# An early expert's result behind the last routing, and expert weights asked for first

## The chip, the cores and the metric

The kernel runs on one core of a Trainium2 chip. A core has a matrix engine (TensorE, PE in the profile; its weight loads are listed as PEld), a vector engine (DVE), a scalar engine (ACT) that evaluates exponents, Gelu and tanh and also copies, a general engine (POOL) that here does small arithmetic and issues the indirect DMAs, and a queue engine (SP) that issues the plain DMAs one after another. Each engine works through its own queue in order, and waits on semaphores for the others. The metric is the device time of one execution in microseconds; lower is better.

## What is computed

Sixteen elements of 112 tokens with 256 features pass through two layers, each an attention and a mixture of eight experts:

```python
x = x + _L0_xattn_ref(_layernorm(x), ctx_1024, ctx_1024, mask, wq, wk, wv, wo)   # 16 heads
x = x + _L0_ffn_ref(_layernorm(x), wr, w1, b1, w2, b2)      # top 2 of 8, capacity 560 an expert
x = x + _L1_xattn_ref(_layernorm(x), ctx_1024, ctx_1024, mask)                 # one head
x = x + _L1_ffn_ref(_layernorm(x), gate_w, w1, w2, w3)      # top 2 of 8, no capacity
```

The change concerns the end of the first attention and the first expert stage. There each token's logits pick two experts; a token's place in an expert's list is the count of earlier tokens that chose it; an expert computes `gelu(x @ w1 + b1) @ w2 + b2` on its rows, and each row's result is weighted by its gate and added to its token.

## The kernel before, in words

All matrix products are in float32. A matmul call of the source shows as two matmuls in the profile.

**First attention with routing beside it.** The work is cut into 64 steps, four for each of the 16 elements; a step does four heads: scores (L712), row minimum (`least`, L720), exponent (`exps`, L727), transposes of the exponents (`turn`, L733 to L739), product with the values (`weigh`, L749). A step's scores, its transposes and its values are done in successive steps, so the pipeline drains in steps 64 and 65. Everything else is hung into the steps by `put(step, place, function, arguments)` (L779): `place` 0, 1 or 2 is one of three points within a step, and functions at the same point run in the order in which they were put. For PE, ACT and DVE this order is fixed by hand (`tc.manual_schedule`, L823). POOL and SP are ordered by the framework's planner, which weighs program order against its own estimate of when operands are there.

After the heads of element b, in steps counted from 4b: `queries_first` (6), `heads_first` (7), `output` (8: output product, residual sum into `x`, statistics and reciprocal standard deviation), `normed2` (9), `routing_T` (10), `logits` and `first_two` (11). Then, for groups of elements (`GROUPS0`; the last two groups are element 14 and element 15 alone), `route_a` (12: one-hot choices and running counts `macc`, tanh of the gate on ACT), `gates` and `route_b` (13: positions by two matmuls, L244 and L245), `to_slots` (13: `dest`, then two indirect scatters of the normalised rows, with gate and token number behind each row, into the experts' slots `xg`). The reciprocal standard deviation is found by three Newton steps (`rstd_of`, L165), on POOL for elements 0 to 14 and on DVE for element 15.

**The early expert.** When ten elements are routed, the least chosen expert is fixed as the first one (`early_choice`). Its first 256 slots are filled by then; step 57 loads them with that expert's bias and weights (`early_loads`), step 64 transposes them (`early_T`), step 65 works out gates (`early_gates`). `early_hidden(f)` computes one of eight chunks of the hidden layer, two of them in each of the steps 66 to 69, and `early_result(j, f0, n)` half of one of two 128-row result tiles, in steps 70 to 73. A finished tile gets its bias and gate on DVE and is added to the tokens by an indirect DMA on POOL.

**The end of the stage.** After the steps, `macc` is summed (`ps_n`, L872), and `in_order` (L301) sorts the remaining experts by their counts: `ids0`, `idn0` (their numbers, read by SP into registers at L299) and the capacities. `terms` (L876) gathers the biases in that order.

**Expert stage.** Pools of this stage (`fp`, `fw`, L884) take the room of those of the attention; `wpool` spans both. The loop at L979 runs over eight experts. For expert `at` it asks SP for the next one's rows and bias (`slots0`, L891), then `w1` and `w2`; it turns its own rows (L913, L914), computes hidden products (`hidden0`, L942) for one or two parts of the rows, and after each part the result of the part before (`result0`, L959 to L964, then an indirect add on POOL). Weights have two buffers for each of `w1` and `w2`: experts with an even number in `wpool`, with an odd one in `fw`. The bias `b2` has two buffers as well. In this stage the planner orders all engines. A load of rows waits until all scatters have landed.

The second layer follows, with an attention and eight experts of its own; the change does not touch its code.

Of the kernel before, what the change touches and what calls it, by code (L numbers as in the profile page):

```python
# [8 lines left out]
F32 = mybir.dt.float32  # L9
# [9 lines left out]
B, S, S2, D = 16, 112, 375, 256  # L19
# [3 lines left out]
FC = F // 128  # L23
# [10 lines left out]
ST = 128  # L34
# [22 lines left out]
def xattn_ffn_kernel(ctx: ExitStack, tc: tile.TileContext, a: dict, out: bass.AP):  # L57
# [107 lines left out]
    def rstd_of(mv, n, pool=False):  # L165

        v = small.tile([S, n], F32, tag=f"var{n}", name="var")
        nc.vector.tensor_scalar(v, mv[:, :, 1], EPS, None, ALU.add)
        r = small.tile([S, n], F32, tag=f"rstd{n}", name="rstd", bufs=4)
        nc.vector.tensor_scalar(r.bitcast(I32), v.bitcast(I32), 1, None, ALU.arith_shift_right)  # L170
        nc.vector.tensor_scalar(r.bitcast(I32), r.bitcast(I32), -1.0, float(0x5F3759DF), ALU.mult, ALU.add)  # L171
        t = small.tile([S, n], F32, tag=f"newton{n}", name="newton")
        if pool:
            for _ in range(3):
                nc.gpsimd.tensor_tensor(t, r, r, ALU.mult)  # L175
                nc.gpsimd.tensor_tensor(t, t, v, ALU.mult)
                nc.gpsimd.tensor_scalar(t, t, -0.5, 1.5, ALU.mult, ALU.add)
                nc.gpsimd.tensor_tensor(r, r, t, ALU.mult)
            return r
        nc.vector.tensor_scalar(v, v, -0.5, None, ALU.mult)  # L180
        for _ in range(3):
            if n == 1:
                nc.vector.scalar_tensor_tensor(t, r, r, v, ALU.mult, ALU.mult)
            else:
                nc.vector.tensor_tensor(t, r, r, ALU.mult)
                nc.vector.tensor_tensor(t, t, v, ALU.mult)
            nc.vector.scalar_tensor_tensor(r, t, 1.5, r, ALU.add, ALU.mult)
        return r
# [154 lines left out]
    with tc.tile_pool(name="aw", bufs=1) as aw, tc.tile_pool(name="ea", bufs=1) as ea, tc.tile_pool(name="ap", bufs=2) as ap, tc.tile_pool(  # L343
# [200 lines left out]
        def output(b):  # L544
            oT = oTs.pop(b)
            ps = bank("ps_o")
            for k in range(KC):
                nc.tensor.matmul(ps[:S, :D], oT[:, k, :], wo[:, k, :], start=(k == 0), stop=(k == KC - 1))
            nc.vector.tensor_tensor(x[:, b, :], ps[:S, :D], x[:, b, :], ALU.add)
            based.append(nc.sync.dma_start(out=xd[b * S : (b + 1) * S, :], in_=x[:, b, :]).ins)  # L550
            mv = small.tile([S, 1, 2], F32, tag="mv2", name="mv2")
            stats(mv, 0, x[:, b, :])
            xn2[b] = mv, rstd_of(mv, 1, b + 1 < B)

        def normed2(b):
            mv, rstd = xn2[b]
# [222 lines left out]
        def put(step, place, f, *args):  # L779
            beside.setdefault((step, place), []).append((f, args))  # L780

        for b in range(B):
            if b:
                at = NG * (b - 1)
                put(at, 0, context_T, b)
                put(at + 1, 0, key_T, b, 0)
                put(at + 1, 2, value, b, 2, 1)
                put(at + 2, 0, key_T, b, 1)
                if b % QB == 0:
                    put(at - 2, 0, layer_norm1, b // QB)  # L790
                    put(at - 1, 0, normed1, b // QB)
                    put(at, 2, query_n, b // QB)
                    put(at + 3, 0, query_T, b // QB)
                put(at + 3, 1, value, b, 0, 2)
            at = NG * b
            put(at + 6, 1, queries_first, b)
            put(at + 7, 2, heads_first, b)
            put(at + 8, 1, output, b)
            put(at + 9, 1, normed2, b)
            put(at + 10, 0, routing_T, b)  # L800
            put(at + 11, 0, logits, b)
            put(at + 11, 1, first_two, b)
        for g, (t0, n) in enumerate(GROUPS0):
            at = NG * (t0 + n - 1) + 12
            put(at, 1, route_a, g)
            put(at + 1, 0, gates, g)
            put(at + 1, 2, route_b, g)
            for j in range(n):
                put(at + 1 + (j if n > 2 else 0), 2, to_slots, t0 + j)
# [3 lines left out]
        put(STEPS - 7, 2, early_loads)  # L813
        put(STEPS, 2, early_T)
        put(STEPS + 1, 2, early_gates)
        for f in range(FC):
            put(STEPS + 2 + f // 2, 2, early_hidden, f)
        for j in range(CAPA // ST):
            for i in range(2):
                put(STEPS + 6 + 2 * j + i, 2, early_result, j, i * FC // 2, FC // 2)  # L820

        engines = {mybir.EngineType.PE, mybir.EngineType.Activation, mybir.EngineType.DVE}
        with tc.manual_schedule(engines=engines):  # L823
            nc.vector.tensor_scalar(nmask, nmask, -1.0, None, ALU.mult)
            layer_norm1(0)
            normed1(0)
            context_T(0)
            key_T(0, 0)
            key_T(0, 1)
            query_n(0)  # L830
            query_T(0)
            value(0, 0, 2)
            value(0, 2, 1)
            got, was = None, None
            for step in range(max(at for at, _ in beside) + 1):

                def place(i):
                    for f, args in beside.get((step, i), ()):
                        f(*args)

                now, was, got = step < STEPS, got, None
                if now:
                    got = scores(step)
                    least(got, 0)
                    least(got, 1)
                if was:
                    turn(step - 1, was, 0)
                if now:
                    exps(got, 0)
                place(0)  # L850
                if now:
                    exps(got, 1)
                    least(got, 2)
                    least(got, 3)
                back = 2 <= step < STEPS + 2
                if back:
                    weigh(step - 2, 0)
                    weigh(step - 2, 1)
                if was:
                    turn(step - 1, was, 1)  # L860
                if now:
                    exps(got, 2)
                place(1)
                if now:
                    exps(got, 3)
                if back:
                    weigh(step - 2, 2)
                if was:
                    turn(step - 1, was, 2)
                place(2)  # L870
            ps = bank("ps_n")
            nc.tensor.matmul(ps[:, :E], ones_, macc[:, B, :], start=True, stop=True)  # L872
            at = in_order(small, ps[:, :E], CAP, caps8[:, 0, :], ids0, idn0, over0, capof0, pick0)
            full = [128, E // 2, FC, E]
            for r in (slice(0, E // 2), slice(E // 2, E)):
                terms = ap.tile(full, F32, tag="s", name="terms", bufs=8)  # L876
                nc.vector.tensor_tensor(
                    terms, at[:, r].unsqueeze(2).to_broadcast(full),
                    b1T.rearrange("p e k -> p k e").unsqueeze(1).to_broadcast(full), ALU.mult,
                )  # L880
                nc.vector.tensor_reduce(b1s[:, r], terms, AX.X, ALU.add)


    with tc.tile_pool(name="fp", bufs=2) as fp, tc.tile_pool(name="fw", bufs=2) as fw, tc.tile_pool(  # L884
# [6 lines left out]
        def slots0(e, r0, rows, own=""):  # L891

            xs = fp.tile([ST, -(-rows // ST) if own else NT, W], F32, tag="xs" + own, name="xs", bufs=1 if own else 2)
            src = of_expert(xg[0:ROWS, :].rearrange("(e r) d -> e r d", e=E), e)
            full = rows // ST
            load = nc.sync.dma_start(
                out=xs[:, :full, :], in_=src[r0 : r0 + full * ST, :].rearrange("(j p) d -> p j d", p=ST)
            )
            after_scatters("xg", load)
            if rows > full * ST:  # L900
                load = nc.sync.dma_start(out=xs[: rows - full * ST, full, :], in_=src[r0 + full * ST : r0 + rows, :])
                after_scatters("xg", load)
            b2 = fp.tile([ST, D], F32, tag="b2" + own, name="b2", bufs=1 if own else 2)
            of = slice(e, e + 1) if isinstance(e, int) else bass.ds(e, 1)
            nc.sync.dma_start(out=b2, in_=a["L0_ffn_b2"][of, :].to_broadcast([ST, D]))
            return xs, b2
# [72 lines left out]
        for at in range(E):  # L979
# [1 line left out]
            todo = CAPS0[at] if at else (CAPB,)  # L981
            rows = sum(todo)
            if at + 1 < E:
                nxt = slots0(who[at + 1], 0, sum(CAPS0[at + 1]))
                pool = wpool if at % 2 else fw
                w1_next = w_in(a["L0_ffn_w1"], who[at + 1], "w1", pool, at + 1)
                w2_next = w_out(a["L0_ffn_w2"], who[at + 1], "w2", pool, at + 1)
            gate, token = weights_of(xs, rows, lambda m: ids0[:m, at : at + 1] if at else idf0[:m])
            xsT = turned0(xs, rows)
# [464 lines left out]
```

## Time and profile before

| what | us |
|---|---|
| median of 3 runs (1166.43 to 1173.64) | 1169.13 |
| profiled execution, its own time | 1165.95 |
| its span, first to last instruction | 1164.2 |
| PE busy, of the span | 1059.8 (91%) |
| DVE, ACT, POOL busy | 476.4, 385.7, 274.6 |
| mean granted PE clock, of full speed | 0.961 |

In the timeline rows of the profile, the first two numbers are the start and the length of a stretch in microseconds from the span's start. Then come the engine, the line of the kernel, the operation, what it writes and reads, the sizes, and how many instructions were merged. Brackets give the engine's idle time before them and what ended it. SPq marks the queue of SP. In rows of the form start:end, the engines' busy times (PE, PEld, DVE, ACT, POOL, with instruction counts) are followed by the granted PE clock, the share of time that the DMA engines were busy, and GB/s. Matmuls are pipelined, so that a busy PE isn't PE at its peak.

### The profile page before, as it was taken

The page shows a single profiled execution, that of the slowest core. Times are in us where ns is not written, and L with a number is a line of the kernel's source. Part 1 is how long each engine was busy: PE and PEld are TensorE (multiplying, and loading weights), DVE is VectorE, ACT ScalarE, POOL GpSimd, SP SyncE. Part 2 cuts the span into 40 slices and gives each one's busy share as a digit, 9 for nine tenths or more (in the row PEclk, how much of TensorE's full clock was granted, in tenths as well). Part 3 has the DMA queues.
Part 4 walks back from the last instruction along what each step waited for, and adds up shares of the span by engine and source line. Part 5 has one row for each costly group of instructions (what it writes and reads, how often), then busy time and mean ns, then how long its engine had stood idle before and what let it go on. Part 6 is the DMA issues. An engine that isn't in the chain of part 4 may idle for free. (4 is left out here: it accounts for less than half of the span.)

```text
span 1164.2 us, 17046 instructions
## 1 busy us (share of the span) xinstructions
PE 1059.8 (91%) x6262; PEld 734.0 (63%) x6262; DVE 476.4 (41%) x1764; ACT 385.7 (33%) x836; POOL 274.6 (24%) x573
## 2 busy tenths in 40 slices
PE   4999999999999959999999777738999999999997
PEld 3666666666666648865667545534868755556665
DVE  1666767767767551211112174562222212212211
ACT  1666666666666503121110154411111110110000
POOL 2011114105122221212223224253213121123231
PEclk9999999999999889999999988958999999999999
DMA  5499931001001225334444321127215222253250
GB/s 144 134 281 197 323 124 38 5 9 39 11 16 52 80 59 160 66 100 109 112 109 112 89 73 49 56 71 213 78 11 148 64 82 59 79 143 88 63 134 17
DMA packets 85008, 110.48 MB, mean 95 GB/s; under 512 B 16881, under 2 KB 76281, under 8 KB 84656
## 3 DMA queue, kind: packets, MB, share of 16 engines
q1 hardware_dynamic: 71152, 92.58, 25.5%
q0 software_dynamic: 13216, 16.15, 8.4%
q8 instruction: 53, 0.87, 0.3%
q10 hardware_dynamic: 544, 0.52, 0.2%
q14 instruction: 43, 0.35, 0.1%
HBM read 77.78 MB, written 46.23 MB: 107 GB/s over the span
## 5 line engine op out<-in xcount | busy, mean ns | idle before, releaser
L1311 PE MATMUL ps_h<-xT,v 128*128 128x384 f32 (+5 forms) x704 | 229.3, 487 | 2.0 <-DVEq L1394 1.0
L1311 PEld LDWEIGHTS ps_h<-xT,v 128*128 128x128 f32 x704 | 134.6, 192 | 92.7 <-issue 54.8
L727 ACT ACTIVATE s<-s,nmx 112x375 f32<-112x375 f32 x256 | 143.2, 603 | 16.1 <-DVE nmx L720 16.1
L720 DVE CUSTOM_DVE_ANT_0 s<-ps_s,nmask 112x375 f32<-112x375 f32 x256 | 127.9, 543 | 38.8 <-PE ps_s L712 37.1
L1319 ACT ACTIVATE si<-ps_h 128x384 f32<-128x384 f32 (+5 forms) x88 | 42.9, 488 | 303.6 <-PE ps_h L1311 268.4
L733 PEld LDWEIGHTS ps_at<-ident,s 112*125 112x125 f32 x768 | 99.0, 188 | 60.2 <-issue 26.0
L733 PE MATMUL ps_at<-ident,s 112*125 112x112 f32 x768 | 133.3, 296 | 3.0 <-ACT s L727 2.4
L1320 DVE TENSOR_TENSOR hT<-ps_h,si 128x384 f32<-128x384 f32 (+5 forms) x88 | 48.8, 554 | 182.6 <-PE ps_h L1311 178.6
L1332 PE MATMUL ps_y<-v,hT 128*128 128x256 f32 (+2 forms) x544 | 119.6, 380 | 0.0
L959 PE MATMUL ps_y<-w,hT 128*128 128x256 f32 (+6 forms) x512 | 115.8, 380 | 0.0
L1332 PEld LDWEIGHTS ps_y<-v,hT 128*128 128x128 f32 (+2 forms) x544 | 100.7, 186 | 16.5 <-issue 0.7
L942 PE MATMUL ps_h<-xsT,w 128*128 128x256 f32 (+8 forms) x320 | 104.7, 488 | 6.8 <-DMA w<-in_L_ffn_w 5.9
L959 PEld LDWEIGHTS ps_y<-w,hT 128*128 128x128 f32 (+6 forms) x512 | 89.8, 179 | 20.3 <-issue 3.4
L284 POOL DMA_INDIRECT xd<-y,token x34 | 51.9, 1527 | 193.9 <-DVE y L964 168.0
L739 ACT COPY aT<-ps_at 125x448 f32<-125x448 f32 x128 | 67.9, 531 | 89.1 <-PE ps_at L733 89.0
L949 ACT ACTIVATE hT<-ps_h,b1s 128x256 f32<-128x256 f32 (+7 forms) x72 | 41.9, 582 | 165.4 <-PE ps_h L942 165.4
L942 PEld LDWEIGHTS ps_h<-xsT,w 128*128 128x128 f32 x320 | 62.1, 199 | 46.5 <-issue 40.6
L175 POOL TENSOR_TENSOR newton<-rstd 112x1 f32<-112x1 f32 (+2 forms) x81 | 15.8, 195 | 304.9 <-DVE rstd L171 202.2
L263 POOL DMA_INDIRECT xg<-xn,dest x64 | 61.0, 954 | 81.3 <-issue 36.3
L284 POOL DMA_INDIRECT yd<-y,token x31 | 48.4, 1562 | 102.1 <-DVE y L1336 93.6
L963 DVE TENSOR_TENSOR y<-ps_y,b 128x256 f32<-128x256 f32 (+6 forms) x32 | 13.5, 423 | 130.0 <-PE ps_y L959 130.0
L749 PE MATMUL av<-aT,v 125*32 125x112 f32 x1536 | 63.4, 267 | 0.9 <-ACT aT L739 0.9
(238 smaller groups left out, 1201.7 us busy)
## 6 DMA issues: line engine op xcount, KB each, us to landing
v<-in_L_ffn_w SPq DMA_DIRECT2D x24, 1024.0 KB
w<-in_L_ffn_w SPq DMA_DIRECT2D x16, 1024.0 KB
xg<-xg SPq DMA_DIRECT2D x7, 1799.0 KB
xg<-zeros SPq DMA_DIRECT2D x1, 7168.0 KB
c<-in_ctx SPq DMA_DIRECT2D x16, 375.0 KB
xg<-zeros SPq DMA_DIRECT2D x1, 1792.0 KB
yd<-zeros SPq DMA_DIRECT2D x1, 1792.0 KB
xd<-x SPq DMA_DIRECT2D x16, 112.0 KB
```

Of the source, the lines that this page charges most:

```text
L263: inst = nc.gpsimd.indirect_dma_start(out=slots[:, :], out_offset=bass.IndirectOffsetOnAxis(ap=rows, axis=0), in_=src, in_offset=None).ins
L284: inst = nc.gpsimd.indirect_dma_start(out=total[:, :], out_offset=bass.IndirectOffsetOnAxis(ap=token, axis=0), in_=y, in_offset=None, comp ...
L720: nc.vector.tensor_tensor_reduce(out=s, in0=ps[i], in1=nmask, scale=1.0, scalar=BIG, op0=ALU.add, op1=ALU.min, accum_out=nmx[:, i : i + 1],)
L727: nc.scalar.activation(got[2][i], got[2][i], AF.Exp, bias=got[1][:, i : i + 1], scale=-1.0)
L733: nc.tensor.transpose(pt[:KT, i * S : (i + 1) * S], s[:, c * KT : (c + 1) * KT], ident[:S, :S])
L739: nc.scalar.copy(aT, src)
L749: nc.tensor.matmul(avs[b][32 * i : 32 * i + 32, n, :], vs[b % 2][:, c, h, :], aT[:, i, :], start=(c == 0), stop=(c == NK - 1),)
L942: nc.tensor.matmul(ps[:, :n], w1[:, k, f * 128 : (f + 1) * 128], xsT[:, k, j0 * ST : j0 * ST + n], start=(k == 0), stop=(k == KC - 1),)
L959: nc.tensor.matmul(ps[:m], hT[:, f, j * ST : j * ST + m], w2[:, f, :], start=(f == 0), stop=(f == FC - 1))
L1311: nc.tensor.matmul(ps[:, :n], w[:, k, f * 128 : (f + 1) * 128], xT[:, k, j0 * ST : j0 * ST + n], start=(k == 0), stop=(k == KC - 1),)
L1320: nc.vector.tensor_tensor(hT[:, f, :n], p3[:, :n], si[:, :n], ALU.mult)
L1332: nc.tensor.matmul(ps[:m], hT[:, f, j * ST : j * ST + m], w2[:, f, :], start=(f == 0), stop=(f == FC - 1))
```

## The change

It has five edits, two of which belong together:

1. The reciprocal standard deviation of element 14 is computed on DVE (as element 15's is).
2. `route_a` of group 5 (element 14) stands ahead of `output(15)` at the same point of step 68, instead of behind it.
3. The eight chunks of `early_hidden` go to steps 65, 66, 67, 68, 68, 69, 69, 70 instead of two to each of 66 to 69; the first to place 1, the others to place 2.
4. `early_result` is computed in two whole tiles behind `in_order`, after all steps, and ahead of `terms`.
5. `b2` gets a third buffer, and the next expert's `w1` is asked for before its rows and bias.

```diff
-            xn2[b] = mv, rstd_of(mv, 1, b + 1 < B)
+            xn2[b] = mv, rstd_of(mv, 1, b + 2 < B)
...
+            if b + 1 == B:
+
+                put(at + 8, 1, route_a, group_of[b - 1])
             put(at + 8, 1, output, b)
...
         for g, (t0, n) in enumerate(GROUPS0):
             at = NG * (t0 + n - 1) + 12
-            put(at, 1, route_a, g)
+            if t0 + n + 1 != B:
+                put(at, 1, route_a, g)
...
-        for f in range(FC):
-            put(STEPS + 2 + f // 2, 2, early_hidden, f)
-        for j in range(CAPA // ST):
-            for i in range(2):
-                put(STEPS + 6 + 2 * j + i, 2, early_result, j, i * FC // 2, FC // 2)
+        for f, (step, i) in enumerate(((1, 1), (2, 2), (3, 2), (4, 2), (4, 2), (5, 2), (5, 2), (6, 2))):
+            put(STEPS + step, i, early_hidden, f)
...
             at = in_order(small, ps[:, :E], CAP, caps8[:, 0, :], ids0, idn0, over0, capof0, pick0)
+            for j in range(CAPA // ST):
+                early_result(j, 0, FC)
...
-            b2 = fp.tile([ST, D], F32, tag="b2" + own, name="b2", bufs=1 if own else 2)
+            b2 = fp.tile([ST, D], F32, tag="b2" + own, name="b2", bufs=1 if own else 3)
...
             if at + 1 < E:
-                nxt = slots0(who[at + 1], 0, sum(CAPS0[at + 1]))
                 pool = wpool if at % 2 else fw
                 w1_next = w_in(a["L0_ffn_w1"], who[at + 1], "w1", pool, at + 1)
+                nxt = slots0(who[at + 1], 0, sum(CAPS0[at + 1]))
                 w2_next = w_out(a["L0_ffn_w2"], who[at + 1], "w2", pool, at + 1)
```

## The prediction, made before the result was known

> **What bounds the kernel now.** I read four views. The busy rows first: TensorE (PE) works 91% of the span, so a gain must come from PE idling, or running at half clock, where the change acts. The groups put 5.9 us of PE idle on the expert weights `w` and 9.4 us on the first expert rows `xs`. The timeline around the hand-over from attention to experts shows the second:
>
> ```profile
> 411.43 0.36 PE L244 MATMUL ps_p<-m,before 112*112 112x8 f32 x2 [1.92 <-DVE m L219]
> ...
> 411.77 0.40 DVE L192 TENSOR_SCALAR xn<-x,mv,rstd 112x256 f32<-112x256 f32 x1
> 412.02 3.48 PE L679 MATMUL ps_eh<-xsT,w 128*128 128x256 f32 x8
> 415.34 0.35 PE L563 MATMUL ps_xT<-ident,xn 112*128 112x112 f32 x2
> 415.53 1.91 PE L692 MATMUL ps_ey<-w,hT 128*128 128x256 f32 x8
> 417.27 0.47 PE L574 MATMUL ps_l<-wrT,xT 128*112 128x8 f32 x4
> 417.60 3.70 PE L692 MATMUL ps_ey<-w,hT 128*128 128x256 f32 x16
> 420.34 0.16 DVE L205 CAST num<-ind 112x2 f32<-112x2 uint32 x1
> ...
> 422.65 0.16 DVE L616 SCALAR_TENSOR_TENSOR dest<-num,pos 112x2 int32<-112x2 f32 x1
> 424.88 0.94 POOL L263 DMA_INDIRECT xg<-xn,dest  x1 [0.30 <-DMA xd<-y,token]
> 426.08 0.16 DVE L325 CAST idn<-ids 1x8 int32<-1x8 f32 x1
> 430.62 0.37 SPq L896 DMA_DIRECT2D xs<-xg  x1
> 433.00 1.07 PE L913 MATMUL ps_t<-ident,xs 128*128 128x128 f32 x4 [9.44 <-DMA xs<-xg]
> 434.57 7.62 PE L942 MATMUL ps_h<-xsT,w 128*128 128x192 f32 x32 [0.49 <-DVE xsT L914]
> ```
>
> The chain that sets the end is the routing of element 15: its row norm is ready at 412.17, but its transposes wait until 415.34 behind two early hidden chunks, its logits and choice behind early result halves, `dest` comes at 422.81, the expert order `idn` at 426.24; SP reads seven expert numbers and asks for `xs` 4.4 us later; PE starts at 433.0. The early result (L692, 7.6 us) thus runs ahead of a 9.4 us hole.
>
> The same timeline in the expert stage, one of three alike places:
>
> ```profile
> 532.03 0.35 SPq L905 DMA_DIRECT2D b<-in_L_ffn_b  x1
> 532.62 0.38 SPq L148 DMA_DIRECT2D w<-in_L_ffn_w  x1
> 539.30 13.55 PE L942 MATMUL ps_h<-xsT,w 128*128 128x496 f32 x32 [1.54 <-DMA w<-in_L_ffn_w]
> ```
>
> SP is one queue. `b2` has two buffers, so its load waits for the previous expert's last result, and the weights stand behind it; they arrive 6.7 us after being asked. The two others idle 2.11 and 2.20 us: 5.85 in all. The clock by stretches:
>
> ```profile
> 398.00:404.80 6.80, 5.35 (x19) 4.64 (x20) 2.50 (x13) 2.54 (x4) 3.46 (x7) 0.50 0.11 34
> 404.80:411.70 6.90, 4.98 (x26) 4.05 (x26) 4.00 (x25) 1.75 (x6) 0.94 (x1) 0.99 0.17 50
> 411.70:415.10 3.40, 3.40 (x10) 2.82 (x11) 1.47 (x10) 1.06 (x4) 0.94 (x1) 0.50 0.02 5
> 428.70:439.00 10.30, 5.51 (x18) 5.00 (x19) 2.78 (x16) 1.03 (x3) 0.00 (x0) 0.50 0.60 118
> ```
>
> The third number from the end is the granted clock: half at 398.0 to 404.8, 411.7 to 415.1 and 428.7 to 439.0.
>
> **Element 14's rstd, from POOL to DVE.** POOL's twelve small steps take 395.63 to 398.86. Element 15's DVE form costs 1.41 us more on DVE (L171 at 409.33, next work at 410.81; for 14 it follows after 0.07). `xn` of 14 starts at 398.2, not 398.9. But everything behind on DVE slips 1.41 us, so ACT's tanh, the copy behind it (`aT`) and the early transposes' copies (`xsT`) end at 398.55, not 397.14.
>
> **First hidden chunk at (65,1).** It needs `xsT`, so PE, free at 395.75, waits to 398.6. Queued behind it on PE: the last weigh, positions of group 4, transposes of 14 and 15. At half clock (as now from 398.0) the chunk takes 1.9 us (two took 3.62), to 400.5. On ACT the Gelu's table load stands ahead of `raw` of 15. The row: load 400.46 to 401.74, and the Gelu at 402.66 waits for PE. ScalarE: Activation LUTs, "What ACT_TABLE_LOAD costs", adds a 1.38 us drain to the 1.28 us load. By the row ACT is ready at 400.0, hidden behind PE; by the rule at 401.4, and `raw` is 0.9 us later. I take the row. `raw` ends about 401.6, transposes of 15 at 403.1 (now 400.9): 2.2 us late. But only one chunk, not two, then stands before its heads, and one before its output: heads at 405.3 (now 405.2), output done 407.2 (now 407.8). Bounds for this step: 0.6 us gained, 0.5 lost if the half clock lasts to 406.
>
> **route_a of group 5 ahead of output(15); chunks spread.** route_a's five steps (0.77 us) move into DVE's wait for `ps_o` (2.25 us at 407.82): free while element 14's logits precede that output. Output, norm and gates of 15 then need 3.5 us, so `xn` is done at 411.0 (now 412.17). PE meanwhile does chunks 3 to 6 (0.95 us each at full clock: 405.01 row) and positions of group 5, ending at 411.2. Transposes of 15 at 411.2 instead of 415.34.
>
> **Early result behind the routing.** Chunk 7 (0.95) covers the copy `xT`; logits at 412.3. DVE's `lg`, maxima, route_a, then PE positions (0.5) and six steps to `dest` (1.2) need 3.5 us with no result tile between: `dest` near 415.8, 7.0 us sooner. The two scatters follow at its heels as now (0.8, then 2.2 us), without the add on POOL; landed (2.6) near 421.3. `idn` needs 2.0 us after `dest` and no longer waits for the second `y`: 417.9, 8.4 us sooner. SP's 4.4 us: `xs` asked for at 422.2, used 2.4 later, 424.6. The result's 7.6 us on PE run from 414.8 to 422.4, in the hole. On DVE the second `y` (0.8), then `terms` (2.1), end at 425.3; queued behind: gate and `xsT` of the first expert (1.5). Hidden products start at 426.9: 7.7 us sooner. POOL's two adds (1.7 each) have only the expert's adds behind them; the first expert's hidden tile lies over the early gates and tokens, so its first Gelu, at 427.9, waits for the last early add, which lands about then (3.9 after issue at 423.6): nothing.
>
> Half clock during the result: PE is idle some 1.3 us and thinly used 2.2 before it; at 409.5 an idle stretch of 1.92 us preceded half clock. At worst it costs 2.5 us, at best nothing; I take 0.4. The first expert: TensorE: Matmul & The Clock Gate, "Why this matters for your kernels", says that only idle gaps above some 3 us bring the half clock back. By it the new gap (2.2 us, transposes, 1.5 us) leaves the clock full, and its 32 matmuls take 5.2 us (0.65 per chunk at 440.28 on) instead of 7.62: 2.4 us gained. The row with the 1.92 us gap says that less suffices. I take the row, nothing gained.
>
> **Weights asked for first; third `b2`.** Of the first weights ahead of `xs` of expert 1: their tile lies over the attention's exponent buffers, which now hold early hidden chunks and `terms`, so SP waits until 425.3, with `xs` behind. `xs` alone took 4.5 us (433.19 to 437.71); with 1 MB ahead, at the 272 GB/s of 460 to 470, 3.9 more: landed 434.5, wanted when the first expert's hidden products end, also 434.5. Between no loss and 3; I take 1. Later, the weights of expert n+1 wait only for the slot freed by expert n-1's hidden products, at least 20 us ahead of use: the 5.85 us go. Next late there: nothing on PE but matmuls. Against it: `xs` now queues behind that slot, and its gate steps, which the planner places early on DVE, block `y` and `xsT` copies if it lands late. Such waits are there already (49.0 us in six, hidden under PE). For experts 3 and 4 `xs` would land about 8 us after the hidden products end, among the `y` steps: 0 to 1.5 us each; I take 0.8 in all. The third buffer itself is 1 KB and no work.
>
> **Sum.** Hand-over 7.7 - 0.4 - 1.0 = 6.3; expert stage 5.85 - 0.8 = 5.05; together 11.4 us. The profiled execution took 1165.95 (span 1164.2, 1.75 around it); it would take 1154.6. That run is 3.2 under the median of 1169.13, so the median becomes 1157.7, 1.0% less; about 1% is what a measurement of this kernel can tell from no change.
>
> **Rivals.** (a) Better: full clock for the first expert, no loss on `xs`: 7.7 + 2.4 + 5.85 = 16, 1153. For: the rule; against: the 1.92 us row. 15%. (b) The wait moves: chunk 0 and half clock hold element 15 up by 2 us and the result runs cold for 2.5, giving 3 + 5 = 8, 1161. 14%. (c) The planner, which orders all engines in the expert stage, already filled the weight waits with a result tile (18 matmuls at 533.69 before the hidden products); its new order gives the gain back by DVE waits on `xs`: 6, 1163. 15%. (d) Slower: those gate waits land ahead of `y` in every expert. Two result buffers of 3.45 us each cover 6.9 us; a landing 10 us late (`xs` took 11.1 us at 459.85) stalls PE 3.2 us, seven times 22, less 6: 16 slower, 1185. It decides once a stall exceeds 0.9 us per expert. Against: hidden products need no DVE, and existing gate waits of 12.5 us stalled nothing. 8%. (e) The change does nothing for the weights, since their slot, not `b2`, binds: SP's own waits name L905 (157 us), so no. Forecast: 48%, 1154 to 1162.
>
> **Numbers.** Half of the forecast's and (a)'s 15% lie beyond 1%, with a little less than that at the edge: faster 0.44, within 1% 0.48, slower 0.08. The range 1152 to 1169 leaves (d) and the extremes of (a) out.
>
> **What would show it.** Right: `dest` of 15 about 7 us sooner, L692 in one piece beside the `xs` wait, which falls from 9.4 to about 2; no PE wait on `w` in the expert stage; `w` ahead of `xs` on SP. Wrong: PE waiting at L679 beyond 399, the half clock across L692, DVE `gate` waits with PE idle behind, or expert 1's transposes waiting for `xs`.

## The result, and the profile after

In 18 runs each, the median is 1164.55 us after the change (1158.80 to 1167.09) against 1171.14 us before (1166.43 to 1176.90). The ratio is 0.9935, with a 95% interval of 0.9920 to 0.9951. That is 7.6 us or 0.65% faster, with an interval of 5.7 to 9.4 us. On the median of 1169.13 that the prediction started from, the ratio makes 1161.5 us, inside its range and 3.8 us above its forecast. The direction was right. The 11.4 us were one and a half times what came, and of the two terms of their sum one was much too large and the other too small.

The profiled execution of after took 1164.5 us, with a span of 1162.8, only 1.4 us less than the span before. Its second layer happened to be slower: from the first transposes of that layer to the end it took 498.2 us, where the profile before has 491.1 and those of the runs below have 490.7 to 496.6, with the same code there. The first half clock of that layer (a stretch in which the granted clock is 0.50) lasted 20.5 us in after and 10.2 in before. So I compare the stages where the change acts, not the spans. The records of one execution also stand later or earlier than those of another: the residual addition of element 14, which lies ahead of all the edits, starts between 390.48 (e4) and 395.15 (e5). I therefore count the hand-over, the passage from the attention to the first expert, from the end of that addition: 394.30 in the trace before, and 395.36 (first row of the second timeline) in the trace after. Two rows of the timeline of before that are needed here, that addition and the second early add:

```profile
393.88 0.42 DVE L549 TENSOR_TENSOR x<-ps_o,x 112x256 f32<-112x256 f32 x1 [0.17 <-PE ps_o L548]
...
426.13 1.72 POOL L284 DMA_INDIRECT xd<-y,token  x1 [0.30 <-DVE ids L324]
```

The timeline of after around the hand-over (start, length, engine, line, operation; lines of the expert stage stand 3 further down than before):

```profile
394.94 0.42 DVE L549 TENSOR_TENSOR x<-ps_o,x 112x256 f32<-112x256 f32 x1 [0.17 <-PE ps_o L548]
...
399.65 2.07 PE L679 MATMUL ps_eh<-xsT,w 128*128 128x256 f32 x4 [2.84 <-ACT xsT L660]
...
412.26 0.38 PE L563 MATMUL ps_xT<-ident,xn 112*128 112x112 f32 x2
...
415.98 8.84 PE L692 MATMUL ps_ey<-w,hT 128*128 128x256 f32 x32
...
416.95 0.16 DVE L616 SCALAR_TENSOR_TENSOR dest<-num,pos 112x2 int32<-112x2 f32 x1
...
418.91 0.16 DVE L325 CAST idn<-ids 1x8 int32<-1x8 f32 x1
...
425.96 1.72 POOL L284 DMA_INDIRECT xd<-y,token  x1 [1.83 <-DVE y L699]
...
430.14 0.37 SPq L899 DMA_DIRECT2D xs<-xg  x1
...
432.50 1.07 PE L916 MATMUL ps_t<-ident,xs 128*128 128x128 f32 x4 [7.68 <-DMA xs<-xg]
...
433.96 6.82 PE L945 MATMUL ps_h<-xsT,w 128*128 128x192 f32 x32 [0.38 <-DVE xsT L917]
```

The early result (L692) is one piece behind the routing, as planned. `dest` of element 15 is ready 6.8 us sooner than before, counted from element 14, and `idn` 8.2 us sooner. And yet SP asks for the first expert's rows (L899) only 1.5 us sooner: 11 us lie between `idn` and that load, where there were 4.4 before. TensorE still waits 7.7 us for `xs`, not about 2.

What held the load is in SP's own waits in that stretch of after (line, what it waited for, total us, times, longest):

```profile
SPq L299 <- DVE more L326: 10.0, 1, 10.0
SPq L899 <- DMA xd<-y,token: 5.9, 1, 5.9
```

L299 is the registers' wait for `idn` (put down to L326, the next instruction of DVE). Behind it the load of the rows waited 5.9 us for the landing of an early add, which POOL had issued at 425.96 (the last row of POOL above). Rows and add have no data in common. They meet in memory: the expert stage's first tile takes the room of the attention's tiles, the second early `y` and its `token` among them. That this first load waits for the last users of that room, the adds among them, is what e5 and e7 below test.

The expert stage, in the timeline of after:

```profile
531.43 0.43 SPq L148 DMA_DIRECT2D w<-in_L_ffn_w  x1
532.05 0.37 SPq L899 DMA_DIRECT2D xs<-xg  x1
...
533.91 0.35 SPq L908 DMA_DIRECT2D b<-in_L_ffn_b  x1
...
561.82 13.04 PE L945 MATMUL ps_h<-xsT,w 128*128 128x480 f32 x32
```

The weights `w1` are asked for 30 us ahead of their use, where it was 6.7 us, and TensorE goes from one product into the next without a pause. In the groups of after (busy us, mean ns, idle us and what ended it) the 5.9 us of waiting for `w` are gone:

```profile
L945 PE MATMUL ps_h<-xsT,w 128*128 128x256 f32 (+8 forms) x320 | 102.1, 478 | 1.2 <-PEq L998 0.8 <-DVE xsT L917 0.4
```

The hidden products of the second expert, of the one behind the third stall (464 rows) and of the eighth, in the timeline of before and then of after:

```profile
444.27 7.14 PE L942 MATMUL ps_h<-xsT,w 128*128 128x256 f32 x32
...
599.60 14.29 PE L942 MATMUL ps_h<-xsT,w 128*128 128x464 f32 x32 [2.20 <-DMA w<-in_L_ffn_w]
...
637.86 11.41 PE L942 MATMUL ps_h<-xsT,w 128*128 128x416 f32 x32 [0.43 <-PEq L995]
```

```profile
443.25 7.17 PE L945 MATMUL ps_h<-xsT,w 128*128 128x256 f32 x32
...
589.36 12.62 PE L945 MATMUL ps_h<-xsT,w 128*128 128x464 f32 x32
...
629.37 11.41 PE L945 MATMUL ps_h<-xsT,w 128*128 128x416 f32 x32 [0.83 <-PEq L998]
```

From the second expert to the eighth before took 193.59 us and after 186.12: 7.5 us less. That is 5.85 us of waits and 1.67 us of half clock: in before a half clock of 3.4 us came behind the third stall, and the products there took 14.29 us, against 12.62 in after.

The clock of after in four stretches (start:end, us, PE busy, granted PE clock, DMA share, GB/s):

```profile
399.20:406.00 6.80, 6.35 (x28) 0.50 0.00 0
411.00:416.30 5.30, 3.78 (x24) 1.00 0.08 23
416.30:419.70 3.40, 3.40 (x10) 0.50 0.23 65
429.90:436.70 6.80, 3.81 (x13) 0.50 0.61 147
```

The third row is a half clock inside the early result, which took 8.84 us for that reason. The last is the half clock that stayed in the first expert's products.

### The profile page after: what moved, and what is told of

It is laid out like the page before. It is cut to its first block, busy times and chain, and to the rows that moved or that the text cites. A ratio compares the mean times of both kernels' runs of the same rounds, so it can differ in the third digit from the quotient of the medians.

```text
span 1162.8 us, 17041 instructions
## 1 busy us (share of the span) xinstructions
PE 1060.9 (91%) x6262; PEld 733.1 (63%) x6262; DVE 477.6 (41%) x1771; ACT 385.9 (33%) x836; POOL 272.1 (23%) x561
## 5 line engine op out<-in xcount | busy, mean ns | idle before, releaser
L727 ACT ACTIVATE s<-s,nmx 112x375 f32<-112x375 f32 x256 | 143.2, 604 | 15.1 <-DVE nmx L720 13.9
L720 DVE CUSTOM_DVE_ANT_0 s<-ps_s,nmask 112x375 f32<-112x375 f32 x256 | 127.9, 543 | 39.1 <-PE ps_s L712 36.4
L945 PE MATMUL ps_h<-xsT,w 128*128 128x256 f32 (+8 forms) x320 | 102.1, 478 | 1.2 <-PEq L998 0.8
L962 PEld LDWEIGHTS ps_y<-w,hT 128*128 128x128 f32 (+6 forms) x512 | 89.7, 179 | 20.5 <-issue 3.4
L284 POOL DMA_INDIRECT yd<-y,token x31 | 48.4, 1561 | 102.1 <-DVE y L1339 93.6
```

Of the source, the lines that this page charges most:

```text
L284: inst = nc.gpsimd.indirect_dma_start(out=total[:, :], out_offset=bass.IndirectOffsetOnAxis(ap=token, axis=0), in_=y, in_offset=None, comp ...
L720: nc.vector.tensor_tensor_reduce(out=s, in0=ps[i], in1=nmask, scale=1.0, scalar=BIG, op0=ALU.add, op1=ALU.min, accum_out=nmx[:, i : i + 1],)
L727: nc.scalar.activation(got[2][i], got[2][i], AF.Exp, bias=got[1][:, i : i + 1], scale=-1.0)
L945: nc.tensor.matmul(ps[:, :n], w1[:, k, f * 128 : (f + 1) * 128], xsT[:, k, j0 * ST : j0 * ST + n], start=(k == 0), stop=(k == KC - 1),)
L962: nc.tensor.matmul(ps[:m], hT[:, f, j * ST : j * ST + m], w2[:, f, :], start=(f == 0), stop=(f == FC - 1))
```

## The experiments

**Theory:** the gain is all in the expert stage, and the hand-over gives next to nothing because the first load into reused memory waits for the landing of the early adds. **Rivals:** the hand-over gained and something else lost it again; SP's registers set the load; the early result, now in the hole, holds the first expert itself.

This table has the hand-over of each profiled execution, in us from the end of element 14's addition: the first expert's rows asked for, its hidden products' start and length, and the start of the second expert's hidden products. The last two columns are the ratio to before and its 95% interval.

| kernel | rows asked | first hidden | its length | second hidden | ratio | interval |
|---|---|---|---|---|---|---|
| before | 36.3 | 40.3 | 7.62 | 50.0 | 1 | |
| after | 34.8 | 38.6 | 6.82 | 47.9 | 0.9935 | 0.9920 to 0.9951 |
| e1, experts only | 36.4 | 40.2 | 7.75 | 49.9 | 0.9935 | 0.9911 to 0.9959 |
| e2, hand-over only | 34.5 | 38.4 | 8.32 | 48.7 | 1.0004 | 0.9989 to 1.0019 |
| e3, third buffer | 36.6 | 40.4 | 7.83 | 50.2 | 0.9952 | 0.9935 to 0.9968 |
| e4, order only | 35.4 | 39.2 | 7.80 | 49.0 | 0.9943 | 0.9920 to 0.9966 |
| e5, second add's memory | 30.8 | 35.9 | 7.66 | 45.5 | 0.9909 | 0.9883 to 0.9935 |
| e7, rows' memory | 25.5 | 35.1 | 7.95 | 45.0 | 0.9901 | 0.9875 to 0.9926 |
| e6, both of these | 27.0 | 33.7 | 8.35 | 44.3 | 0.9886 | 0.9861 to 0.9911 |
| e8, first add's memory too | 26.7 | 32.0 | 5.44 | 44.2 | 0.9885 | 0.9860 to 0.9909 |
| e9, e8's memory, old order | 33.2 | 38.1 | 6.90 | 48.4 | 0.9927 | 0.9901 to 0.9953 |
| e10, e8 with rows first | 26.8 | 32.1 | 5.44 | 41.6 | 0.9867 | 0.9849 to 0.9885 |

Where an expectation below gives a time "after the output of element 14", it counts from the start of that addition, so that its figure is 0.4 us larger than the table's. A row of the table is one execution, and a half clock that falls differently can shift it by 1 or 2 us (last section). The intervals of e5, e7 and e9 overlap with that of after, so what one moved tile does is read from the traces; by their times, only e6, e8 and e10 are clear of after.

### One part of the change alone

e1 is before with edit 5 alone:

```diff
-            b2 = fp.tile([ST, D], F32, tag="b2" + own, name="b2", bufs=1 if own else 2)
+            b2 = fp.tile([ST, D], F32, tag="b2" + own, name="b2", bufs=1 if own else 3)
...
-                nxt = slots0(who[at + 1], 0, sum(CAPS0[at + 1]))
                 pool = wpool if at % 2 else fw
                 w1_next = w_in(a["L0_ffn_w1"], who[at + 1], "w1", pool, at + 1)
+                nxt = slots0(who[at + 1], 0, sum(CAPS0[at + 1]))
```

> The kernel before with the expert-stage edit alone (third bias buffer, weights ahead of rows). Theory (all of the gain is in the expert stage; the hand-over gives nothing because the first load of rows waits for the last early add): the three waits on w (5.85 us) go, and with the third of them the half clock that followed it (13.9 us products took 14.29 instead of 12.62: 1.7 us); 7.5 us faster, ratio 0.9936, the first expert's hidden products as late as before (434.6 plus or minus 1). Rival (both parts pay about half): 3 to 4 us faster, ratio 0.997.

e2 is after with edit 5 undone, the same lines the other way round:

> The kernel after with the expert-stage edit undone: only the hand-over edits (DVE root, order of route_a, spread chunks, early result behind the routing). Theory: the chain of element 15 ends some 6 us sooner, but the first rows are asked for at about 430 as before, 4.1 us after the last early add is issued; 0 to 1 us faster, ratio 0.999 to 1.000, three PE waits on w of about 6 us together. Rival (the hand-over pays): rows asked for before 427, 3 to 6 us faster, ratio 0.995 to 0.997.

e1 took 1157.44 us and e2 1163.48, where before took 1164.31 (e1 to e4 ran on one chip). e1 has the whole gain, 0.9935, and e2 none that can be measured. (The "13.9 us products" in the expectation of e1 are the products of 464 rows, 12.62 us at full clock.) The groups of e1 first, then those of e2, show why:

```profile
L942 PE MATMUL ps_h<-xsT,w 128*128 128x256 f32 (+8 forms) x320 | 103.0, 482 | 1.0 <-PEq L995 0.5 <-DVE xsT L914 0.4
```

```profile
L945 PE MATMUL ps_h<-xsT,w 128*128 128x256 f32 (+8 forms) x320 | 105.5, 491 | 6.6 <-DMA w<-in_L_ffn_w 5.8 <-PEq L998 0.4 <-DVE xsT L917 0.4
```

In e2 the waits on `w` are back, 5.8 us of them, and so is a half clock behind one of them (565.0 for 3.4 us). Its rows are asked for at 425.67 in its own trace, which looks like the rival's "before 427", but that trace stands 3.2 us earlier than the one before: on its count they are asked for at 428.8, 4.27 us behind the second add. Its second expert starts 1.3 us sooner than in before. The runs can't tell those 1.3 us from nothing, since e2's interval allows 1.3 us of gain and 2.2 of loss.

e3 (the first two lines of e1's diff: the third buffer) and e4 (its other lines: weights ahead of rows, with two buffers) divide edit 5:

> The kernel before with the third bias buffer alone; rows are still asked for ahead of the weights. Theory (the bias load was the only thing that held the weights up on the SP queue): no PE wait on w, 7.5 us faster, ratio 0.9936. Rival (the order does it): rows in front keep the weights late, PE waits on w of 3 us or more stay, ratio above 0.996.

> The kernel before with the weights asked for ahead of rows and bias, two bias buffers as before. Theory: the bias load then stands behind w1 and ahead only of w2, which waits for the same last result anyway; no PE wait on w, 7.5 us faster, ratio 0.9936, as good as the third buffer. Rival (the buffer is needed): the weights of the expert after next are held up by the bias load and PE waits on w stay at about 6 us, ratio 0.999.

They took 1158.38 and 1157.20 us, and neither waits for `w` any more. Either half is enough. The stalls need both conditions at once, a load that waits for a buffer and the weights queued behind that load. Taking the wait away or standing ahead of it cures the same thing, and the two together gave no more than one.

### The memory that the first load reuses

These three kernels are after with tiles moved elsewhere. e5 takes the second add out of the reused room: the second result and the tokens get memory of their own, and `terms` stands ahead of the result.

```diff
-            token = early["token"] = ea.tile([ST, CAPA // ST], I32, name="token")
+            token = early["token"] = const.tile([ST, CAPA // ST], I32, name="token")
...
-                y = ap.tile([128, NG * S], F32, tag="aT", name="y", bufs=4)[:, :D]
+                y = zeros if j else ap.tile([128, NG * S], F32, tag="aT", name="y", bufs=4)[:, :D]
...
-            for j in range(CAPA // ST):
-                early_result(j, 0, FC)
...
-                terms = ap.tile(full, F32, tag="s", name="terms", bufs=8)
+                terms = ap.tile(full, F32, tag="qT", name="terms")
...
+            for j in range(CAPA // ST):
+                early_result(j, 0, FC)
```

e7 takes the load out of it: the first expert's rows go to the room of the input `x`. e6 does both.

```diff
+            if r0 == CAPA and not own:
+                xs = xpool.tile([ST, -(-rows // ST), W], F32, tag="x", name="xs")
...
```

> The kernel after, with the second early result tile and the tokens of the early rows in memory of their own, and the two products of terms computed ahead of the early result. Nothing is left out; the same two adds are issued at the same place. Theory (the first load of expert rows is the first user of memory that the attention stage used, and waits for all its last users; the last of them is the landing of the second early add, 4.2 us after its issue): the second add no longer counts, so the barrier becomes the first add, issued some 3 to 3.5 us earlier; the rows are asked for about 3.5 us sooner relative to the output of element 14 (35.2 us after it in the kernel after), hidden products of the first expert start some 3 us sooner, and the ratio to before is about 0.990 to 0.992 against 0.9935. Rival (SP's seven expert numbers and the scatters set the load, or the gap on TensorE is closed by something else anyway): the rows are asked for at most 1 us sooner, ratio 0.9935 as now.

> The same, and the first expert's rows go into the tile that held the input x, so that their load waits for the scatters only. Nothing is left out. Theory: the rows are asked for once SP has read its seven numbers and the scatters have landed, about 29 us after the output of element 14 instead of 35.2; the first tile written in the reused room by DVE still waits for the first add; hidden products of the first expert start 4.5 to 6 us sooner than in the kernel after, ratio to before about 0.988 to 0.990. Rival (the early result of 7 us on TensorE and its two sums on DVE, moved behind the routing, now hold the first expert): asked for sooner, but hidden products at most 1 us sooner, ratio 0.9935.

> The kernel after, with the first expert's rows alone in the tile that held the input x; the early result is as in the kernel after. Nothing is left out. Theory: the rows are asked for about 29 us after the output of element 14 and are there early, but the next user of the reused room (the expert's b2, then DVE's gate and the transposed rows) still waits for the landing of the second add, so hidden products start only about 2 to 3 us sooner than in the kernel after: ratio to before about 0.991 to 0.992. Rival (only the load itself was held): hidden products 4.5 to 6 us sooner, ratio 0.988 to 0.990, as in the run with all three changes.

They took 1160.20, 1156.60 and 1157.67 us, where before took 1171.02 in their runs. In the timeline of e5 the rows are asked for 4.1 us after the first add is issued, and the second add no longer counts:

```profile
422.26 1.63 POOL L284 DMA_INDIRECT xd<-y,token  x1 [3.11 <-DVE y L699]
...
425.02 1.59 POOL L284 DMA_INDIRECT xd<-zeros,token  x1 [1.13 <-DVE zeros L699]
...
426.36 0.37 SPq L899 DMA_DIRECT2D xs<-xg  x1
...
431.43 7.66 PE L945 MATMUL ps_h<-xsT,w 128*128 128x192 f32 x32 [0.48 <-DVE xsT L917]
```

So the load is 4.0 us sooner than in after, as the theory had it. SP still reads all seven registers before this load, so the registers are not what held it.

The timeline of e7 shows the other side. The rows are asked for 9.3 us sooner, 3 us more than I had expected (the load now stands ahead of five of the registers, which the first expert doesn't need), but the next user of the reused room waits in their place. That is the expert's bias load, and on DVE the gate:

```profile
418.75 0.37 SPq L904 DMA_DIRECT2D xs<-xg  x1
...
422.60 1.72 POOL L284 DMA_INDIRECT xd<-y,token  x1 [1.83 <-DVE y L699]
...
426.85 0.22 DVE L936 SCALAR_TENSOR_TENSOR gate<-xs,idf 128x1 f32<-128x1 f32 x1 [2.58 <-DMA xd<-y,token]
...
428.32 7.95 PE L950 MATMUL ps_h<-xsT,w 128*128 128x192 f32 x32 [5.63 <-DVE xsT L922]
```

The gate starts 4.25 us after the second add was issued, and DVE's idle time is put down to that add. Of the 9.3 us, 3.5 reach the hidden products. I had expected 2 to 3, and a ratio of 0.991 to 0.992; the measured 0.9901 is a little better, with an interval that covers the expectation. In e6, which has both and starts the hidden products 4.9 us sooner, as expected, the same wait is there for the first add (timeline of e6):

```profile
418.97 0.37 SPq L904 DMA_DIRECT2D xs<-xg  x1
...
420.04 1.63 POOL L284 DMA_INDIRECT xd<-y,token  x1 [3.11 <-DVE y L699]
...
424.37 0.22 DVE L936 SCALAR_TENSOR_TENSOR gate<-xs,idf 128x1 f32<-128x1 f32 x1 [3.54 <-DMA xd<-y,token]
...
425.61 8.35 PE L950 MATMUL ps_h<-xsT,w 128*128 128x192 f32 x32 [3.44 <-DVE xsT L922]
```

In these kernels the first user of the room that has to wait starts 4.1 to 4.5 us after the last add that still counts was issued (the early adds of before landed 4.0 us after their issue): 4.49 in before, 4.18 in after, 4.27 in e2, 4.10 in e5, 4.25 in e7, 4.33 in e6.

### No add left, and what comes late next

e8 is e6 with the first result and the first expert's rows in one tile in the room of the input. e9 has the same memory with edits 1 to 4 undone, so the early result stands ahead of the routing again and the other edits of the hand-over are gone with it.

```diff
+                if j == 0:
+                    early["room"] = xpool.tile([128, B * D], F32, tag="x", name="room")
-                y = zeros if j else ap.tile([128, NG * S], F32, tag="aT", name="y", bufs=4)[:, :D]
+                y = zeros if j else early["room"][:, B * D - D :]
...
-                xs = xpool.tile([ST, -(-rows // ST), W], F32, tag="x", name="xs")
+                n = -(-rows // ST)
+                xs = early["room"][:, : n * W].rearrange("p (j d) -> p j d", j=n)
```

> The kernel after with the memory of all early tiles moved: the first early result and the first expert's rows in the room of the input x, the second result and the tokens in memory of their own, terms ahead of the result. Nothing is left out. Theory (landing of the adds was the barrier): with no add left among the last users, the first expert waits for its rows and for the last early product only; hidden products start 31 to 32.5 us after the output of element 14 (39.0 in the kernel after, 34.1 with one add still counted), ratio to before 0.985 to 0.988. Rival (the early result behind the routing holds the first expert by itself): hidden products not before 34 us, ratio 0.989 as with one add still counted.

> The same memory, but the work in the order of the kernel before: early result ahead of the routing of element 15, early products two to a step (the expert stage as in the kernel after). Nothing is left out. Theory: moving the result is worth something once the adds no longer bind: the routing is 6.8 us later here, so the first expert's hidden products start 5 to 6 us later than in the kernel with the result behind the routing, at 37 to 38.5 us, ratio to before 0.990 to 0.993. Rival (the order of the result never mattered, only the memory): within 2 us of the other, ratio 0.985 to 0.988.

e8 took 1151.78 us and e9 1156.30, where before took 1164.12. The timeline of e8:

```profile
424.25 0.70 PE L924 MATMUL ps_t<-ident,room 128*128 128x128 f32 x4 [0.52 <-DVE zeros L700]
...
425.09 0.22 DVE L939 SCALAR_TENSOR_TENSOR gate<-room,idf 128x1 f32<-128x1 f32 x1 [0.51 <-DVE zeros L701]
...
426.33 5.44 PE L953 MATMUL ps_h<-xsT,w 128*128 128x192 f32 x32 [1.38 <-DVE xsT L925]
...
435.34 0.83 PE L924 MATMUL ps_t<-ident,xs 128*128 128x128 f32 x4 [3.14 <-DMA xs<-xg]
```

No add stands in the waits, and the first expert follows the early result with 0.52 and 1.38 us of idle time on TensorE. Its products start at 32.0 us, at the late end of what was expected, and run at full clock, in 5.44 us. The ratio, 0.9885, just misses the expected 0.985 to 0.988 and is not better than e6's: TensorE now waits 3.14 us for the rows of the second expert, which stand behind 1 MB of `w1` in SP's queue and are 8 us under way. Both kernels reach the second expert at the same time.

e9 answers whether the edits of the hand-over, the move of the result above all, are worth anything once the memory is free. Its timeline, for DVE, SP and PE:

```profile
419.97 0.16 DVE L616 SCALAR_TENSOR_TENSOR dest<-num,pos 112x2 int32<-112x2 f32 x1
...
424.90 0.37 SPq L904 DMA_DIRECT2D room<-xg  x1
...
429.81 6.90 PE L950 MATMUL ps_h<-xsT,w 128*128 128x192 f32 x32 [0.43 <-issue]
```

With the late routing, the rows wait for the scatters and are asked for 6.5 us later than in e8. The second expert starts 4.1 us later, and the ratios differ by 0.0042, or 4.9 us; from the spread of the six runs of each I estimate 1.5 to 8 us. So with the memory free, edits 1 to 4 together are worth about 4 to 5 us; with the adds in the way, e2 found nothing. What the place of the result is worth without the other three edits no run shows.

e10 is e8 with the first part of edit 5 alone: the third buffer stays, and the rows stand ahead of `w1` again.

```diff
-                w1_next = w_in(a["L0_ffn_w1"], who[at + 1], "w1", pool, at + 1)
                 nxt = slots0(who[at + 1], 0, sum(CAPS0[at + 1]))
+                w1_next = w_in(a["L0_ffn_w1"], who[at + 1], "w1", pool, at + 1)
```

> The run with all early tiles' memory moved, and of the change's last part only the third bias buffer: the rows of the next expert are asked for ahead of its w1 again. Nothing is left out. Theory (with the first expert's products early and at full clock, the rows of the second expert, 8 us under way behind 1 MB of w1, are what TensorE waits for, 3.1 us): the rows land some 4.5 us after they are asked for, that wait goes, hidden products of the second expert start 41 to 42.5 us after the output of element 14 instead of 44.7, no wait on w comes back, ratio to before 0.985 to 0.9875. Rival (w1 itself then is late, or w1 and the rows share the same bandwidth): the wait changes its name to w and hidden products start at 44 us or later, ratio 0.9885 or more.

It took 1149.32 us, where before took 1164.06: ratio 0.9867, 15.5 us faster than before, with an interval of 13.4 to 17.6. That is twice the gain of the change and the best of the ratios, though its interval and e8's overlap. The timeline of e10:

```profile
426.88 5.44 PE L953 MATMUL ps_h<-xsT,w 128*128 128x192 f32 x32 [1.37 <-issue]
...
433.04 0.63 PE L924 MATMUL ps_t<-ident,xs 128*128 128x128 f32 x4 [0.72 <-DMA xs<-xg]
...
436.34 7.14 PE L953 MATMUL ps_h<-xsT,w 128*128 128x256 f32 x32 [0.95 <-DMA w<-in_L_ffn_w]
```

The wait for rows falls from 3.14 to 0.72 us. I had said that no wait on `w` would come; 0.95 us of one did, but the second expert starts 2.6 us sooner all the same.

## Why the prediction was partly right

Its steps, with the times after taken back by the 1.06 us between the two traces:

- **Element 14's rstd and chunk 0: right.** Predicted from 398.6 to 400.5; it ran from 398.6 to 400.7. The row was the better guide for the table load: in the trace after, it took ACT from 399.80 to 401.08 and the Gelu began at 401.76, when the chunk ended. The further 1.38 us that the prediction quotes beside the row would not have fitted in, in front or behind.
- **Element 15 and the routing: right.** Transposes 411.2 (measured 411.2), `dest` 415.8 (416.1), `idn` 417.9 (418.0).
- **Half clock across the result: under-sized.** I took 0.4 us of a possible 2.5. L692 took 8.84 us in after and 7.15 at full clock in e2, so 1.7; a half clock there was one of the signs that I had named for being wrong. `terms` ended 1.3 us later than said. Nor was it hidden: DVE waited 2.64 us for the end of L692 before the second `y`, so that the second add, and the load behind it, came up to 1.7 us later than at full clock. (e2 had the full clock, but its result started 1.4 us later, so that its rows are asked for only 0.3 us sooner than those of after.)
- **"`xs` asked for at 422.2": this step failed.** It was asked for at 429.1. I made `idn` and seven registers the bound, and wrote that POOL's two adds have only the expert's adds behind them and cost "nothing". I had seen that the expert stage's tiles lie over the early tokens, but placed that wait at the first hidden tile. It stands at the first load into the room. The early result that I moved behind the routing took its add with it: from 426.13 to 425.96 in the two traces, 1.2 us sooner from element 14. So `xs` came only 1.5 us sooner. In before, six of the seven registers were read by 429.7 (the seventh came behind the load; the prediction counts all seven ahead of it), and the add landed at about 430.1, 4.0 us after its issue: the two nearly coincided, which hid the add. From the load on, my steps held: 2.4 us from asking to use.
- **Half clock in the first expert: right by luck.** It came back, with 6.82 us for those products, but behind a gap of 7.7 us that I had not foreseen. Behind the short gaps of e8 and e10 the clock stayed full, which speaks for the rule that I had set aside; a gap of the 2.2 us in my sum, no run has there.
- **Rows of the second expert behind `w1`, a loss of 1.0: not in after** (0.19 us). In e8 it is 3.14 us, about the upper bound of that step, once the first expert's products came early. The bound was right for a kernel in which the rest of the sum had come true.
- **Expert stage: 5.05 said, 7.5 in the trace.** All 5.85 us of waits went, the 0.8 us for late rows never came, and 1.67 us of half clock went with the stalls, which the sum had left out. The run with edit 5 alone gives 7.6 us.
- **Hand-over: 6.3 said, 2.1 in the trace** for the second expert's start, part of it a shorter half clock (6.82 instead of 7.62). Measured, e1 and after have the same ratio, so it is nothing that can be told from zero.
- **The total: inside the range, partly by luck.** The range was 17 us wide, and the 2.5 us that the expert stage gave beyond its term made up for part of what the hand-over didn't give. The remark that a measurement can tell about 1% was too cautious: 18 runs each give 0.65% with some 0.16% on either side.

Of the rivals, (b) has the nearest number (8 us) but not its mechanism: element 15 wasn't held up. It does contain the slower result. (c) and (d) did not occur; DVE still waits for rows at its gate steps, and TensorE loses nothing by it. (e) is excluded by e1. (a), the full clock for the first expert, came only in e8 and e10.

What stays open is whether after's hand-over is worth 0 or 2 us. The traces say 1.3 to 2.1, of which a different fall of the half clock may be a part; the runs say none, and their intervals are wider than the difference.

## What to carry to other kernels

When work is moved behind a hand-over, ask what its last instruction is and whose memory it holds: here an add that the next step doesn't read was the last user of a room whose next tile was on the critical path, and the wait for its landing, over 4.1 to 4.5 us after its issue, took the place of the wait removed. Move the tile of such a last user or of the first newcomer elsewhere, and move both, since the second newcomer waits as well. When one queue carries a load that waits for a buffer ahead of a large one, cure either of the two, and count with the stalls the half clock that can follow one of them: here one stall of three, in before and in e2.

## What the runs showed of the hardware

The half clock didn't follow the length of TensorE's idle gap alone. Ahead of the early result the gap was 1.52 us in after and in e2 alike. In after the half clock came and the result took 8.84 us; in e2, whose timeline is this, it didn't:

```profile
412.47 0.36 PE L244 MATMUL ps_p<-m,before 112*112 112x8 f32 x2 [1.52 <-DVE m L219]
...
413.11 7.15 PE L692 MATMUL ps_ey<-w,hT 128*128 128x256 f32 x32
```

In e6 it was full as well, and in e5, e7, e8 and e10 half again, always for 3.4 us, with gaps of 1.52 or 1.53 us each time.

The traces show what differed. In each of them, all changes of the granted clock lie a whole number of 3.413 us apart (the half-clock stretches of the hand-over are 3.4, 6.8, 10.2 or 13.7 us long), so that a beat can be laid through the whole execution. In the five traces with half clock, the gap lay whole within one beat (in after from 413.82 to 415.35, in the beat from 412.85 to 416.26), and the next beat was the half one. In e2 and e6 the end of a beat cut the gap into 0.46 and 1.06 us and into 0.38 and 1.14 us, and the clock stayed full. The stalls on `w` agree. In before they were 1.54, 2.11 and 2.20 us long, and only the third left as much as 2.0 us idle in one beat; in e2 they were 1.38, 2.18 and 2.28 us long, and only the second did, with 2.1. Behind these two the half clock came, and behind the other four, with at most 1.3 us in one beat, it didn't.

After and e2 have the same code up to there, so where the beat falls differs from one execution to the next, and 1.7 us between two single profiles of the early result can be the beat alone. How much idle time a beat bears is not one number: in before, after and e1, beats at the end of the early result's dense products had 1.77, 1.68 and 1.85 us idle and the next beat kept the full clock; in e3 and e4 they had 2.03 and 2.00, and it lost it. Among the small products of the routing 1.52 us were enough.

The Trainium skill (TensorE: Matmul & The Clock Gate, "Why this matters for your kernels") speaks of gaps above about 3 us. It names them as what to avoid, and doesn't say that shorter ones are safe, as the prediction read it. Behind gaps of 0.5 and 1.4 us the first expert ran at full clock (e8, e10), and behind 3.4 us or more at half (e6, e7, after), as it says. The 1.52 us of after, and the 2.2 us of two stalls, are under it, and half clock came all the same; there the measurement decides.
